# Rows of b2 spread by GpSimd, and a new order of the first twenty microseconds, in a conditional residual kernel

## The chip, the cores and the metric

The kernel runs on one core of a Trainium2 chip. The metric is device time in microseconds of one execution. Three executions of the kernel before took 303.17, 303.27 and 303.47; the median, 303.27, is the time before.

The engines are called as in the profile: PE is TensorE, DVE is VectorE, ACT is ScalarE, POOL is GpSimd, SP is SyncE. A "q" behind a name is that engine's instruction queue (its sequencer), which also issues DMAs.

## The reference

For each of 128 batches there is a tile x[b] of 128 rows and 512 columns, float32, and a language id 0 to 8 that picks one of ten sets of weights.

```python
h = relu(einsum('bsh,bha->bsa', x, W1[lang]) + b1[lang])      # 512 -> 128
adapted = einsum('bsa,bah->bsh', h, W2[lang]) + b2[lang]      # 128 -> 512
y = x + adapted
mean, var = mean(y), var(y)                                   # over the 512 columns
normed = (y - mean) * rsqrt(var + 1e-5)
out = x + normed * gamma[lang] + beta[lang]
```

The ids are data: which row of b2, gamma or beta a batch needs is known on the chip only.

## The kernel before, in words

Each batch is one 128x512 tile, and the main loop goes over batches with its stages shifted against each other. Every instruction is chained behind the one before it on its own engine (`keep`, L46), so the order of the calls in the text is the order on each engine, and a wait holds up all that stands behind it there.

A batch takes these steps:

- `transpose_x` (L264, the matmuls at L271 into pxT): four transposes of x on PE. `copy_xT` (L273) brings them to SBUF by ACT. There is one pxT buffer. The first 17 batches read strided columns.
- `down` (L290, ph at L294): x times W1 on PE, with the batch's W1 in a tile w1s. `relu` (L300) by ACT gives hT.
- `up` (L304, py at L311): h times W2 on PE into one of five y buffers in PSUM (`p_y`, which the rows below use too). For a batch of `b2_by_matmul` one more product (L310) picks its row of b2 out of `parts` and adds it on PE.
- b2 comes in by one of three ways: by that product; by VectorE, which adds the row of the table `b2_b` to y (`vector_b2`, L318, for the batches of `b2_by_vector`); or by GpSimd, which adds it to x beforehand (`add_b2`, L277, tile r). `add_beta` (L283, tile o) adds beta's row to x on GpSimd for every batch.
- `residual` (L323) on VectorE adds x or r to y and sums; `square` on ACT sums squares; `scale` and `finish` (L394, L403) on VectorE apply mean, gamma and the root and write o; `store` sends two batches at a time. A y buffer is free after `finish`, so `up` of batch b + 5 needs `finish` of batch b.

W1 reaches w1s in two ways. For batches 0 to 16 `load_first` (L158) loads the batch's own W1 from DRAM, after reading the id into a register; from batch 17 on, `stage_w1` (L259) copies it on ACT out of `w1`, the whole table, loaded in four parts by `load_w1`. W2 is loaded in two parts (`load_w2`): languages 0 to 2, then 3 to 9; an `up` waits for both. x of batches 0 to 19 comes two batches a load (`load_part`), later four batches a load (`load_x`, in the main loop). DMAs count on eight semaphores in turn, so each issue waits until the eighth load before it has landed.

Before the main loop stands the opening, an order written out by hand (L540 to L581). Beta, gamma and b2, ten rows each, are loaded into `rows`, split into two bf16 parts in `parts`, and spread over all 128 partitions into the tables `beta_b`, `gamma_b`, `b2_b` (10 x 512 columns each) in two ways:

- `spread(r, engine)` (L225): a matmul by a one-hot column writes row r to all partitions of a y buffer, and ACT copies it to the table (L232).
- `four_copies` (L238) makes one tile with the 30 rows in each group of 32 partitions, and `shuffle_rows` (L244) has VectorE spread row r out of it by a shuffle within each group (L247).

Rows 0 to 9 are beta, 10 to 19 gamma, 20 to 29 b2. `spin` runs matmuls on a constant whose result nobody reads. `x_turn` is `transpose_x` and `copy_xT` together. After the loop stands a second order by hand for the last batches.

Of the kernel before, what the change touches and what calls it, by code (L numbers as in the profile page):

```python
# [8 lines left out]
FP = mybir.dt.float32  # L9
# [7 lines left out]
P = 128  # L17
G = 4
# [4 lines left out]
U = 2  # L23
# [3 lines left out]
def cond_resid_kernel(ctx: ExitStack, tc: tile.TileContext, x, itok, W1, b1, W2, b2, gamma, beta, out):  # L27
# [8 lines left out]
    nc = tc.nc  # L36
# [40 lines left out]

    ids = const.tile([1, B], I32, name="ids")
    rows = rp.tile([P, H], FP, tag="r", name="rows")
    b1r = const.tile([L, A], FP, name="b1r")  # L80
    w1 = const.tile([P, L, KC, A], FP, name="w1")
    w2 = const.tile([P, L * H], FP, name="w2")
# [3 lines left out]
    def load_part(lo, hi, engine=nc.sync):  # L86
        dst = xs[lo // G][:, lo % G : lo % G + hi - lo, :]
        keep(engine.dma_start(out=dst, in_=x[lo:hi].rearrange("b s h -> s b h")))
# [2 lines left out]
    keep(nc.vector.memset(warm, 1.0))  # L91

    keep(nc.sync.dma_start(out=ids, in_=itok.rearrange("(o b) -> o b", o=1)))
    keep(nc.scalar.dma_start(out=rows[0:L, :], in_=beta))
    keep(nc.sync.dma_start(out=rows[L : 2 * L, :], in_=gamma))
    keep(nc.scalar.dma_start(out=rows[2 * L : 3 * L, :], in_=b2))
    load_part(0, 2)
    keep(nc.scalar.dma_start(out=b1r, in_=b1))
    keep(nc.scalar.activation(warm, warm, AF.Abs_reciprocal_sqrt))

    def load_w1(k):
        keep(
            nc.sync.dma_start(out=w1[:, :, k, :], in_=W1[:, k * P : (k + 1) * P, :].rearrange("l p a -> p l a"))
        )
# [53 lines left out]
    def load_first(b):  # L158
        w1s[b] = wp.tile([P, KC, A], FP, tag="w1s", name=f"w1s_{b}")
        src = W1[bass.ds(lid(b, ET.SP), 1)].rearrange("o (p k) a -> p (o k a)", k=KC)  # L160
        keep(nc.sync.dma_start(out=w1s[b].rearrange("p k a -> p (k a)"), in_=src))  # L161

    def load_w2(lo, hi):
        dst = w2[:, lo * H : hi * H].rearrange("p (l h) -> p l h", l=hi - lo)
        keep(nc.sync.dma_start(out=dst, in_=W2[lo:hi].rearrange("l a h -> a l h")))
# [1 line left out]
    load_w2(0, 3)  # L167
    load_first(0)
    load_first(1)
    load_part(2, 4)  # L170
    load_first(2)
    load_first(3)
    load_w2(3, L)
    xs[1] = xp.tile([P, G, H], FP, tag="x", name="x_1")
    load_part(4, 6)
# [21 lines left out]
    xs[4] = xp.tile([P, G, H], FP, tag="x", name="x_4")  # L197
    load_part(16, 18)
    load_w1(2)
    load_first(16)  # L200
    load_part(18, 20)
    load_w1(3)

    def upper(lo):

# [14 lines left out]

    beta_b = const.tile([P, L * H], FP, name="beta_b")
    gamma_b = const.tile([P, L * H], FP, name="gamma_b")
    b2_b = const.tile([P, L * H], FP, name="b2_b")

    def spread(r, copier):  # L225
        t = (beta_b, gamma_b, b2_b)[r // L]
        row = p_y.tile([P, H], FP, tag="y", name=f"row_{r}")
        pick_r = pick[:, r : r + 1].to_broadcast([96, P])
        keep(nc.tensor.matmul(row, lhsT=pick_r, rhs=parts[:96, :], start=True, stop=True))  # L229
        dst = t[:, r % L * H : (r % L + 1) * H]  # L230
        if copier is nc.scalar:
            keep(nc.scalar.copy(dst, row))  # L232
        else:
            keep(nc.vector.tensor_copy(dst, row))
# [3 lines left out]
    def four_copies():  # L238
        t = p_y.tile([P, H], FP, tag="y", name="four_p")
        keep(nc.tensor.matmul(t, lhsT=sel, rhs=parts[:96, :], start=True, stop=True))  # L240
        fours[0] = rp.tile([P, H], FP, tag="r", name="four")
        keep(nc.vector.tensor_copy(fours[0], t))

    def shuffle_rows(lo, hi):  # L244
        for r in range(lo, hi):
            t = (beta_b, gamma_b, b2_b)[r // L]
            keep(nc.vector.stream_shuffle(t[:, r % L * H : (r % L + 1) * H], fours[0], [r] * 32))  # L247

    xT, hT, rs, os, ys, ssqs, nmeans, rstds = {}, {}, {}, {}, {}, {}, {}, {}
    phs, pxs, sums = {}, {}, {}  # L250


    def b2_by_matmul(b):
        return b in (0, 1) or b >= B - 2

    def b2_by_vector(b):
        return b in (2, 3, 9, 13, 17, 21) or 24 <= b < B - 8 and (b % 16 in (1, 6, 11) or b % 32 == 30)

    def stage_w1(b):  # L259
        w1s[b] = wp.tile([P, KC, A], FP, tag="w1s", name=f"w1s_{b}")  # L260
# [22 lines left out]
    def add_beta(b):  # L283
        g, j = divmod(b, 2)
        if j == 0:
            os[g] = op.tile([P, 2, H], FP, tag="o", name=f"o_{g}")
        v = lid(b, ET.Pool)
        keep(nc.gpsimd.tensor_tensor(os[g][:, j, :], xb(b), beta_b[:, bass.ds(v * H, H)], ALU.add))  # L288

    def down(b):  # L290
        phs[b] = p_h.tile([P, P], FP, tag="h", name=f"ph_{b}")
        for k in range(KC):
            keep(
                nc.tensor.matmul(  # L294
                    phs[b], lhsT=w1s[b][:, k, :], rhs=xT[b][:, k, :], start=(k == 0), stop=(k == KC - 1)
                )
            )
        del xT[b], w1s[b]
# [110 lines left out]
    def on(b):  # L409
        return 0 <= b < B  # L410
# [125 lines left out]
    def x_turn(b):  # L536
        transpose_x(b)
        copy_xT(b)

    spin(7, H)  # L540
    four_copies()
    spread(10, nc.scalar)
    spin(1, H)
    x_turn(0)
    transpose_b1()
    spread(11, nc.scalar)
    for n in (0, G):
        lid(n, ET.PE)
    shuffle_rows(0, 10)
    x_turn(1)  # L550
    spread(12, nc.scalar)
    spread(13, nc.scalar)
    down(0)
    relu(0)
    spread(14, nc.scalar)
    x_turn(2)
    spread(15, nc.scalar)
    down(1)
    relu(1)
    spread(16, nc.scalar)  # L560
    spread(17, nc.scalar)
    x_turn(3)
    down(2)
    relu(2)
    spread(18, nc.scalar)
    spread(19, nc.scalar)
    add_beta(0)
    add_beta(1)
    spread(20, nc.scalar)
    spread(21, nc.scalar)  # L570
    down(3)
    relu(3)
    spread(22, nc.scalar)
    add_beta(2)
    add_beta(3)
    shuffle_rows(23, 30)
    spin(1, H)
    spin(1, H // 2)
    up(0)
    x_turn(4)  # L580
    up(1)  # L581

    turned = 5
    for i in range(3, B - 6):
        b = i - U - 1
        if b > G and b % G == 2 and b // G + 3 < NG and b // G + 3 >= 5:
            load_x(b // G + 3)
        up_to = i
        if b <= E:
            if turned <= up_to and on(turned):  # L590
                transpose_x(turned)
            add_b2(b + 2)
            if 4 <= b + 2 <= E:
                add_beta(b + 2)
        for n in range(turned, min(B, up_to) + 1):
            if on(n) and (n > turned or b > E):
                transpose_x(n)
            down(n - 1)
            if on(n):
                copy_xT(n)  # L600
            relu(n - 1)
            if on(n + 1) and n + 1 >= FIRST:
                stage_w1(n + 1)
        turned = max(turned, min(B, up_to) + 1)
        if i - U >= 2 and on(i - U):
# [225 lines left out]
```

## Time and profile before

| what | us | where from |
|---|---|---|
| median of three executions | 303.27 | times |
| the profiled execution | 303.5 | times |
| its span | 301.7 | page |
| busy PE, DVE, ACT, POOL | 294.0, 294.1, 278.9, 281.2 | page, part 1 |
| median from issue to landing: x of two batches, w1s, last part of W2 | 7.1, 7.7, 10.1 | page, part 6 |
| longest waits before 25 us: POOL for beta, PE for x, DVE for PE's up | 11.6, 1.0, 1.0 | waits |
| one spread on ACT (L232), one shuffle on DVE (L247) | 0.59, 0.74 | timeline |
| add of 128x512 on POOL, first and last in the loop | 1.27, 1.46 | timeline |

PE's granted clock is 1.0 in the record throughout. Busy time of an instruction includes what overlaps the next one, so a step's cost in a row of equal instructions is the distance between their starts: 0.65 for a shuffle that records 0.74, 1.23 for an add on GpSimd that records 1.27 or more.

### The profile page before, as it was taken

The numbers are of one execution on the slowest core, as the hardware profiler recorded it, in microseconds if no ns is written. First come the engines' busy times: TensorE is split into PE (matmuls) and PEld (weight loads), VectorE is DVE, ScalarE is ACT, GpSimd is POOL, SyncE is SP. The second block draws the span as 40 slices with busy tenths as digits, with TensorE's granted clock in tenths as the row PEclk, the third lists the DMA queues.
The fourth block names the chain that finished last, engine by engine and source line by source line (L and its number), as shares of the span: only waits on it lengthen the run. The fifth ranks groups of instructions, "written<-read, shape, count | busy, mean of one in ns | idle before, by whom it ended". The sixth has DMA issues, their size and how long they took to land.

```text
span 301.7 us, 7025 instructions
## 1 busy us (share of the span) xinstructions
PE 294.0 (97%) x1829; PEld 219.4 (73%) x1829; DVE 294.1 (97%) x785; ACT 278.9 (92%) x770; POOL 281.2 (93%) x236
## 2 busy tenths in 40 slices
PE   7899999999999999999999999999999999999993
PEld 3668777777777777777777777777777777777761
DVE  6979999999999999999999999999999999999996
ACT  5878789999999999999999999999999999999983
POOL 1299998999999999999999999999999999999972
PEclk9999999999999999999999999999999999999999
DMA  6999999986658866766777566778766667872826
GB/s 232 387 387 366 347 339 406 405 298 193 245 223 268 279 225 219 234 234 236 249 276 244 200 231 241 253 237 277 261 191 219 249 228 249 277 258 98 278 93 224
DMA packets 45353, 78.11 MB, mean 259 GB/s; under 512 B 2137, under 2 KB 9316, under 8 KB 45314
## 3 DMA queue, kind: packets, MB, share of 16 engines
q1 hardware_dynamic: 45254, 77.62, 74.4%
q8 instruction: 15, 0.25, 0.4%
q14 instruction: 24, 0.20, 0.2%
q10 hardware_dynamic: 60, 0.05, 0.1%
HBM read 44.11 MB, written 33.55 MB: 257 GB/s over the span
## 4 chain that ended last, share of the span: by engine, by line
PE 89%; DVE 5%; issue 2%; DMA 2%; SPq 0%; POOL 0%; DVEq 0%; POOLq 0%
PE ph L294 36%; PE py L311 35%; PE pxT L271 18%; DMA x<-in_x_dram 2%; DVE py L328 1%; DVE o L488 1%; DVE py L394 1%; PE row L229 1%; DVE n L494 0%; SPq L161 0%; PE py L310 0%; SPq L143 0%; PE idle L529 0%; DVE rstd_of L370 0%; DVEq L826 0%
## 5 line engine op out<-in xcount | busy, mean ns | idle before, releaser
L288 POOL TENSOR_TENSOR o<-x,beta_b 128x512 f32<-128x512 f32 x121 | 163.1, 1380 | 12.6 <-DVE beta_b L247 11.6
L294 PE MATMUL ph<-xT,w1s 128*128 128x128 f32 x1024 | 135.4, 275 | 0.2 <-DMA w1s<-in_L_cond_W_dram 0.2
L311 PE MATMUL py<-w,hT 128*128 x256 | 131.3, 595 | 0.0
L281 POOL TENSOR_TENSOR r<-x,b_b 128x512 f32<-128x512 f32 x92 | 127.1, 1382 | 0.0
L294 PEld LDWEIGHTS ph<-xT,w1s 128*128 128x128 f32 x1024 | 124.9, 192 | 1.9 <-issue 0.9
L271 PEld LDWEIGHTS pxT<-ident,x 128*128 128x128 f32 x512 | 65.9, 149 | 66.6 <-issue 49.9
L394 DVE SCALAR_TENSOR_TENSOR py<-py,nmean,gamma_b 128x512 f32<-128x512 f32 x124 | 93.5, 754 | 0.0
L403 DVE SCALAR_TENSOR_TENSOR o<-py,rstd,o 128x512 f32<-128x512 f32 x116 | 86.8, 748 | 0.0
L351 ACT ACTIVATE sq<-py,sum 128x512 f32<-128x512 f32 x124 | 85.9, 693 | 0.8 <-DVE py L328 0.6
L275 ACT COPY xT<-pxT 128x512 f32<-128x512 f32 x128 | 74.7, 584 | 5.3 <-PE pxT L271 5.1
L271 PE MATMUL pxT<-ident,x 128*128 128x128 f32 x512 | 77.6, 274 | 1.2 <-DMA x<-in_x_dram 1.0
L328 DVE SCALAR_TENSOR_TENSOR py<-py,r 128x512 f32<-128x512 f32 x97 | 67.1, 692 | 0.1
L262 ACT COPY w1s<-w 128x512 f32 x108 | 66.1, 612 | 0.0
L302 ACT ACTIVATE hT<-ph,b1T 128x128 f32<-128x128 f32 x128 | 47.0, 367 | 8.6 <-PE ph L294 4.2
L311 PEld LDWEIGHTS py<-w,hT 128*128 128x128 f32 x256 | 39.1, 192 | 1.5 <-issue 0.7
L351 ACT ACTIVATION_READ_ACCUMULATOR sq<-py,sum 128x1 f32 x124 | 25.1, 202 | 0.0
L328 DVE SCALAR_TENSOR_TENSOR py<-py,x 128x512 f32<-128x512 f32 x31 | 21.7, 699 | 1.8 <-PE py L311 1.0
L321 DVE TENSOR_TENSOR py<-py,b_b 128x512 f32<-128x512 f32 x27 | 18.7, 693 | 0.1
L361 ACT ACTIVATE root<-ssq,eps 128x2 f32<-128x2 f32 x62 | 16.5, 265 | 0.0
L328 DVE DVE_READ_ACCUMULATOR py<-py,r 128x1 f32 x97 | 13.8, 142 | 0.0
L342 ACT ACTIVATE nmean<-sum 128x2 f32<-128x2 f32 x61 | 12.1, 199 | 0.0
L370 DVE SCALAR_TENSOR_TENSOR rstd<-part,root 128x2 f32<-128x2 f32 x62 | 9.4, 152 | 0.0
(73 smaller groups left out, 105.8 us busy)
## 6 DMA issues: line engine op xcount, KB each, us to landing
out_dram<-o SPq DMA_DIRECT2D x62, 512.0 KB, 3.4
x<-in_x_dram SPq DMA_DIRECT2D x27, 1024.0 KB, 6.6
x<-in_x_dram SPq DMA_DIRECT2D x10, 512.0 KB, 7.1
w1s<-in_L_cond_W_dram SPq DMA_DIRECT2D x20, 256.0 KB, 7.7
w<-in_L_cond_W_dram SPq DMA_DIRECT2D x4, 640.0 KB, 8.2
w<-in_L_cond_W_dram SPq DMA_DIRECT2D x1, 1792.0 KB, 10.1
w<-in_L_cond_W_dram SPq DMA_DIRECT2D x1, 768.0 KB, 5.3
out_dram<-o SPq DMA_DIRECT2D x4, 128.0 KB, 1.7
```

The costliest lines, as they stand in the source:

```text
L262: keep(nc.scalar.copy(w1s[b].rearrange("p k a -> p (k a)"), src))
L271: keep(nc.tensor.transpose(pxs[b][:, k, :], cols, ident))
L275: keep(nc.scalar.copy(xT[b], pxs.pop(b)))
L281: keep(nc.gpsimd.tensor_tensor(rs[b], xb(b), b2_b[:, bass.ds(v * H, H)], ALU.add))
L288: keep(nc.gpsimd.tensor_tensor(os[g][:, j, :], xb(b), beta_b[:, bass.ds(v * H, H)], ALU.add))
L294: nc.tensor.matmul(phs[b], lhsT=w1s[b][:, k, :], rhs=xT[b][:, k, :], start=(k == 0), stop=(k == KC - 1))
L302: keep(nc.scalar.activation(hT[b], phs.pop(b), AF.Relu, bias=b1T[:, bass.ds(lid(b, ET.Activation), 1)]))
L311: keep(nc.tensor.matmul(ys[b], lhsT=hT[b], rhs=w2[:, bass.ds(v * H, H)], start=not m, stop=True))
L328: nc.vector.scalar_tensor_tensor(ys[b], ys[b], 1.0, r, ALU.mult, ALU.add, accum_out=col(sums, b))
L351: nc.scalar.activation(sq, ys[b], AF.Square, bias=col(sums, b), scale=-float(H), accum_out=col(ssqs, b))
L394: nc.vector.scalar_tensor_tensor(ys[b], ys[b], col(nmeans, b), gamma_b[:, bass.ds(v * H, H)], ALU.add, ALU.mult)
L403: nc.vector.scalar_tensor_tensor(o, ys[b], rstds[g][:, j : j + 1], o, ALU.mult, ALU.add)
```

## The change

The ten rows of b2 are loaded a second time, as one row of 5120 numbers in partition 0 of `b2_b`, and GpSimd spreads them to all partitions with two `partition_broadcast` instructions of 2560 columns. So `spread` and `shuffle_rows` no longer handle rows 20 to 29. In the built program GpSimd changes its instruction library ahead of the two broadcasts, and changes it back ahead of its first add.

The opening is reordered: x of 0 and 1 is the first load of ACT's queue, and the three loads into `rows` go to SP; x of 2 and 3 is issued behind the w1s of 2 and 3; seven rows go by `spread` (before: thirteen) and thirteen by `shuffle_rows` (before: seventeen); `up` of 0 and 1 both stand ahead of `x_turn(4)`, and `up` of 2 follows it. b2 of batches 0 and 7 is added by VectorE (before: by PE and by GpSimd). In the main loop x of 20 to 23 is issued two batches sooner, ahead of the store of batches 4 and 5. The last part of `w1` is issued ahead of two loads that stood before it. Nothing else of the loop, and nothing of the last order by hand, is touched.

```diff
@@ loads @@
-    keep(nc.scalar.dma_start(out=rows[0:L, :], in_=beta))
+    load_part(0, 2, nc.scalar)
+    keep(nc.sync.dma_start(out=rows[0:L, :], in_=beta))
+    keep(nc.scalar.dma_start(out=b1r, in_=b1))
+    keep(nc.scalar.dma_start(out=b2_b[0:1, :], in_=b2.rearrange("(o l) h -> o (l h)", o=1)))
     keep(nc.sync.dma_start(out=rows[L : 2 * L, :], in_=gamma))
-    keep(nc.scalar.dma_start(out=rows[2 * L : 3 * L, :], in_=b2))
-    load_part(0, 2)
-    keep(nc.scalar.dma_start(out=b1r, in_=b1))
+    keep(nc.sync.dma_start(out=rows[2 * L : 3 * L, :], in_=b2))
...
     load_first(1)
-    load_part(2, 4)
     load_first(2)
     load_first(3)
+    load_part(2, 4)
     load_w2(3, L)
...
     load_w1(2)
+    load_w1(3)
     load_first(16)
     load_part(18, 20)
-    load_w1(3)
@@ b2 @@
+    for half in range(2):
+        cols = slice(half * (L // 2) * H, (half + 1) * (L // 2) * H)
+        keep(nc.gpsimd.partition_broadcast(b2_b[:, cols], b2_b[0:1, cols]))
...
     def b2_by_matmul(b):
-        return b in (0, 1) or b >= B - 2
+        return b in (1,) or b >= B - 2
     def b2_by_vector(b):
-        return b in (2, 3, 9, 13, 17, 21) or 24 <= b < B - 8 and (b % 16 in (1, 6, 11) or b % 32 == 30)
+        return b in (0, 2, 3, 7, 9, 13, 17, 21) or 24 <= b < B - 8 and (b % 16 in (1, 6, 11) or b % 32 == 30)
@@ the opening, as it stands after @@
+    spin(7, H)
+    transpose_b1()
+    for n in (0, G):
+        lid(n, ET.PE)
+    x_turn(0)
+    spin(1, H)
+    spread(2, nc.scalar)
+    four_copies()
+    shuffle_rows(3, 4)
+    spread(0, nc.scalar)
+    shuffle_rows(6, 7)
+    x_turn(1)
+    spread(13, nc.scalar)
+    shuffle_rows(9, 10)
+    shuffle_rows(4, 5)
+    spread(1, nc.scalar)
+    down(0)
+    relu(0)
+    shuffle_rows(17, 18)
+    shuffle_rows(11, 12)
+    shuffle_rows(8, 9)
+    spread(12, nc.scalar)
+    shuffle_rows(7, 8)
+    shuffle_rows(5, 6)
+    add_beta(0)
+    add_beta(1)
+    spin(1, H)
+    x_turn(2)
+    down(1)
+    relu(1)
+    shuffle_rows(18, 19)
+    x_turn(3)
+    shuffle_rows(15, 16)
+    spread(19, nc.scalar)
+    down(2)
+    relu(2)
+    spread(10, nc.scalar)
+    down(3)
+    relu(3)
+    up(0)
+    up(1)
+    x_turn(4)
+    up(2)
+    shuffle_rows(14, 15)
+    add_beta(2)
+    shuffle_rows(16, 17)
@@ the main loop @@
-        if b > G and b % G == 2 and b // G + 3 < NG and b // G + 3 >= 5:
-            load_x(b // G + 3)
+        if b == 8 or b > 12 and b % G == 2 and b // G + 3 < NG:
+            load_x(5 if b == 8 else b // G + 3)
...
-            if 4 <= b + 2 <= E:
+            if 3 <= b + 2 <= E:
                 add_beta(b + 2)
...
-        if i - U >= 2 and on(i - U):
+        if i - U >= 3 and on(i - U):
             up(i - U)
```

More of the change, by code (lines that the diff above doesn't have):

```diff
@@ L79, in cond_resid_kernel @@
     rows = rp.tile([P, H], FP, tag="r", name="rows")
+    b2_b = const.tile([P, L * H], FP, name="b2_b")
     b1r = const.tile([L, A], FP, name="b1r")
@@ L222, in cond_resid_kernel @@
     gamma_b = const.tile([P, L * H], FP, name="gamma_b")
-    b2_b = const.tile([P, L * H], FP, name="b2_b")
     def spread(r, copier):
@@ L540, in cond_resid_kernel @@
     spin(7, H)
[L541 to L544, printed above, removed]
     transpose_b1()
-    spread(11, nc.scalar)
     for n in (0, G):
         lid(n, ET.PE)
-    shuffle_rows(0, 10)
+    x_turn(0)
[5 more added lines that the diff above has]
+    shuffle_rows(6, 7)
     x_turn(1)
-    spread(12, nc.scalar)
     spread(13, nc.scalar)
+    shuffle_rows(9, 10)
+    shuffle_rows(4, 5)
+    spread(1, nc.scalar)
     down(0)
     relu(0)
-    spread(14, nc.scalar)
+    shuffle_rows(17, 18)
[7 more added lines that the diff above has]
+    spin(1, H)
     x_turn(2)
-    spread(15, nc.scalar)
     down(1)
     relu(1)
-    spread(16, nc.scalar)
-    spread(17, nc.scalar)
+    shuffle_rows(18, 19)
     x_turn(3)
+    shuffle_rows(15, 16)
+    spread(19, nc.scalar)
     down(2)
     relu(2)
[L565 to L570, printed above, removed]
+    spread(10, nc.scalar)
     down(3)
     relu(3)
-    spread(22, nc.scalar)
-    add_beta(2)
[L575 to L581, printed above, removed]
+    up(0)
[3 more added lines that the diff above has]
+    shuffle_rows(14, 15)
+    add_beta(2)
+    shuffle_rows(16, 17)
     turned = 5
```

## The prediction

> **What bounds the kernel now.** Times are microseconds from the span's start. I read the busy table first (PE 97%, DVE 97%, ACT 92%, POOL 93%), which names no bound. Then the chain of waits: PE takes 89% of it, and cut to 10 to 24 us it has no gap of another engine:
>
> ```profile
> 4.73 5.58 DMA x<-in_x_dram
> 10.31 0.14 issue
> 10.44 0.72 PE pxT L271 x4
> ...
> 16.58 0.31 PE py L310
> 16.89 0.94 PE py L311 x2
> 17.83 0.71 PE pxT L271 x4
> 18.54 0.22 PE py L310
> 18.76 1.72 PE py L311 x4
> 20.48 0.47 PE pxT L271 x4
> 20.94 0.89 PE ph L294 x8
> ```
>
> Columns: start, length, what. PE waits once for x of batches 2 and 3 (landed at 10.31) and never rests again; from 20.94 on a batch is ph 0.89, py 0.86, pxT 0.47, 2.22 together (2.19 from batch 17 on, where the transposes read whole columns). So the span is the opening up to the ph of batch 4 at 20.94, then 124 steps of a fixed size, then the tail. Only a shift of that 20.94, or a new wait behind it, changes the time.
>
> Next the DMA side, from the table of issues (median to landing) and SyncE's timeline (start, length):
>
> ```profile
> w<-in_L_cond_W_dram SPq DMA_DIRECT2D x1, 1792.0 KB, 10.1
> ```
>
> ```profile
> 1.52 0.41 SPq L88 DMA_DIRECT2D x<-in_x_dram  x1
> 1.97 0.47 SPq L165 DMA_DIRECT2D w<-in_L_cond_W_dram  x1
> 6.24 0.44 SPq L165 DMA_DIRECT2D w<-in_L_cond_W_dram  x1
> 6.72 0.61 SPq L88 DMA_DIRECT2D x<-in_x_dram  x1
> ```
>
> The second part of W2 lands at 6.24 + 10.1 = 16.34, and no up can start before it, whatever PE does. The engines' windows give the DMA 151 GB/s in 0 to 5 us and about 388 from 5 to 25: the queue is full from about 3.3 us on, so a landing moves only with the front of the queue or with its place in it.
>
> Last GpSimd and VectorE, from their timelines:
>
> ```profile
> 13.06 4.98 POOL L288 TENSOR_TENSOR o<-x,beta_b 128x512 f32<-128x512 f32 x4 [11.60 <-DVE beta_b L247]
> ...
> 22.91 1.29 POOL L281 TENSOR_TENSOR r<-x,b_b 128x512 f32<-128x512 f32 x1
> ```
>
> ```profile
> 16.80 0.76 DVE L247 STREAM_SHUFFLE b_b<-four 128x512 f32<-128x512 f32 x1
> ...
> 29.55 0.69 DVE L328 SCALAR_TENSOR_TENSOR py<-py,r 128x512 f32<-128x512 f32 x1
> ```
>
> GpSimd idles until beta is spread (13.06) and then runs without a gap, an add every 1.23 us. It is busy, but ahead: its r of batch 6 ends at 24.20 and VectorE uses it at 29.55, a lead of 5.35. Leads of the same kind are 6.2 at batch 4, 4.8 at batch 8 and 3.8 at batch 90, the least. VectorE is also near full, with five y buffers between it and PE; in the early batches a buffer is free about 0.5 us or more before the up that needs it.
>
> **The change, part by part.**
>
> *The front of the queue.* x of 0 and 1 is issued at about 0.75 (ScalarE's first issue) instead of 1.52: at most 0.77 earlier. Behind it ScalarE issues b1 and the new 20 KB row of b2 (20 KB at 388 GB/s: 0.05). SyncE now issues ids, beta, gamma and b2 ahead of W2's first part: one issue more, so that part starts near 2.2 instead of 1.97. x takes 512 KB / 390 GB/s = 1.3 us to move, which covers the 0.25. The first w1s now waits for x of 0 and 1 to land, because it reuses that load's semaphore (eight go round): about 4.3 instead of 3.77; W2's first 768 KB (2.0 us) cover that, barely. The bounds of the shift are -0.25 (SyncE's later issue sets the front) and 0.77 (all of it); I take 0.65, nearer the upper end since the transfer that opens the queue is the one that moves. W2 then lands at 15.7.
>
> *x of 2 and 3 behind two w1s.* 2 x 256 KB more ahead of it: 1.35 later, less 0.65: 11.0 instead of 10.31. From there PE has pxT 0.47, ph 0.89, pxT 0.47, row 0.22, ph 0.89, row 0.22, ph 0.89 = 4.05, done at 15.05, before W2. So the six spreads taken from PE (13 to 7, 0.22 each), the half spin and the b2 product of batch 0 (0.22) are not counted as such: they let PE be ready, and the landing of W2 takes over as the limit. Without that cover each would be worth its 0.22.
>
> *up of 1 ahead of pxT of 4.* From W2 on: up 0.94, row 0.22, up 0.86, pxT 0.47, up 0.86, pxT 0.47 = 3.82. With 0.05 for the start, ph of batch 4 begins at 15.75 + 3.82 = 19.57 instead of 20.94: **1.37 earlier**. x of 4 and 5, which PE waited for at 17.79 before, lands near 17.1 and is wanted at 17.77. w1s of 4 (landed 18.43 before) is there too.
>
> *VectorE.* parts comes some 0.45 later, since the last of the three row loads is issued at 1.87 on SyncE instead of 1.38; four is copied by 6.7 instead of 5.87. Then 13 shuffles at 0.65 instead of 17, ending at 15.1; the last beta row is the ninth, 12.6. All before the first up ends at 16.7. b2 of batch 0 adds 0.70: 16.7 to 17.4, residuals of 0 and 1 to 19.1, up of 2 ends at 19.1: just covered; uncovered it would cost up to 0.7. b2 of batch 7 is 0.70 more where VectorE runs 0.11 behind PE; batch 9 makes the same step today (0.77 behind) and PE does not wait; the 0.5 of free buffers hides it, 0.2 per batch is caught up.
>
> *The broadcasts.* No row shows one. The b2 row, behind x on ScalarE's queue, lands near 4.6. Each broadcast writes 2560 elements per partition. From rows: memset of 128x128 against 128x1 (0.20, 0.10) is 0.8 ns an element, 4.2 us for both; the two-input add (1.27 for 512) is 2.5 ns, 12.7 us for both. The select of ident, one input, is 1.5 ns; between it and the memset I take 6 us. They end at 10.6, and 17.3 at worst. The instruction needs another GpSimd library, changed ahead of the broadcasts and back ahead of the first add. The row on such a change:
>
> ```profile
> masks.py:199 POOLq MODIFY_POOL_CONFIG  x2: 11/11/11, 1.1 to 1.1; - x2
> ```
>
> 11 ns, and the select begins 0.06 after it. It may ask for a library that is already there, so it bounds the change from below only; from above the nearest row is ScalarE's table load, 1.28. I take a few tenths. GpSimd then starts adding when beta is there, at 12.7 as before, with one add less (batch 7). When would it hurt? The lead of 5.35 less the 1.4 that PE gains: free until 13.06 + 5.35 - 1.4 = 17.0, 0.5 more for the y buffers, then one for one; at 18.9 the whole gain is gone. Later batches allow more (batch 90: 3.8, plus 1.23 for batch 7, plus a wait of 1.0 for a store at 46 us that a late GpSimd absorbs).
>
> Here the Trainium skill speaks against the change: its page "GPSIMD Engine Reference", section 2.1, says the first call to a freshly loaded kernel also pays a load of about 6 us (5.95 measured) that the profile shows as no instruction. The trace neither confirms nor excludes it, since it holds no change to a library that was not there. An estimate by that page: 1.5 + 5.95, 6 for the broadcasts, 5.95 back, adds from 19.4, and the time 303.8.
>
> *x of 20 and w1.* x of 20 to 23 was issued at 43.09 and landed near 53.2, with the transposes of 20 at 53.53: 0.3 to spare. Moved ahead of one 512 KB store it lands 1.3 + 0.65 earlier, PE wants it 1.37 earlier: 0.9 to spare. The store it passes (landed near 50) frees an output buffer that GpSimd next writes at 56. w1's last part passes w1s of 16 and x of 18, which come 640 KB, 1.6 us, later and had over 5 to spare. Nothing.
>
> **Sum.** 301.7 - 1.4 = 300.3. The profiled execution took 303.5, 1.8 beside its span, and lies 0.23 above the median of 303.27; on the median the forecast is **301.9**.
>
> **Rivals.**
> *The front does not move* (SyncE's issue order holds it): W2 lands at 16.34, gain 0.7, 302.6. For it: the w1s that waits; against: 1.3 us of x as cover. 0.08.
> *x of 20 does not come sooner*, so PE waits at 53 us and keeps 0.3 of the gain: 303.0. For it: the queue is full to 60 us; against: its place in the queue. 0.07.
> *GpSimd starts late*: place, the first add of beta after the broadcasts; it decides from 18.9 on. Two-input speed for the broadcasts and a table load's 1.28 at each library change: 4.6 + 12.7 + 2.6 = 19.9; VectorE waits at the r of batch 6, 19.9 - 17.5 = 2.4 less 1.4: 1.0 slower, 304.3. For it: no row shows the operation, both library changes are new, the DMA is full while code would load; against: the configuration row and the one-input rates. 0.33, of which 0.05 lands within 0.6 us of before.
>
> **How the numbers follow.** The forecast has 0.52. Within 0.2% (0.6 us) is what the measurement cannot tell from no change. Faster: 0.52 + 0.08 = 0.60; same: 0.07 + 0.05 = 0.12; slower: 0.28. The forecast's own range, with the shift from -0.25 to 0.77 and 0.3 for the covers, is 301.4 to 302.8; stretched over the late GpSimd it is 301.4 to 304.4, leaving out a still later GpSimd and little else.
>
> **What would show it.** Right: first up near 15.7, ph of batch 4 near 19.6, steps of 2.22 and 2.19 after it without a PE gap, GpSimd's first beta add near 12.7. Wrong: an empty stretch on GpSimd around the broadcasts, beta adds from 17 on, VectorE waiting for r at batches 4 to 8; or W2 landing at 16.3; or PE waiting for x at batch 20.

## The result, and the profile after

The changed kernel takes 313.14 us, the median of five executions (312.73 to 313.92), beside 303.47 for the kernel before on the same chip: 9.7 us more (9.9 between the two profiled spans, 311.6 and 301.7), a ratio of 1.0324 with a 95% interval of 1.0313 to 1.0335. The forecast of 301.9 was wrong, and its range of 301.4 to 304.4 too.

In the chain of work that ended last PE had 89%. It now has 58%, and VectorE, GpSimd and time without a visible cause ("issue") stand in the rest:

```profile
PE 58%; DVE 13%; POOL 13%; issue 10%; DMA 1%; POOLq 1%; ACT 1%; DVEq 0%; SPq 0%; ACTq 0%
```

Where the 9.7 us lie is seen on GpSimd first. Its timeline in the changed kernel (start, length, what; in brackets the idle time before it and the event that ended nearest to its end):

```profile
1.41 0.29 POOL masks.py:199 TENSOR_SCALAR_AFFINE_SELECT ident<-ident 128x128 f32<-128x128 f32 x1 [0.29 <-POOL eps L113]
9.72 5.48 POOL L252 PARTITION_BROADCAST b_b<-b_b  x2 [8.02 <-DVE four L243]
25.93 4.94 POOL L293 TENSOR_TENSOR o<-x,beta_b 128x512 f32<-128x512 f32 x4 [10.73 <-ACT sq L356]
30.83 1.25 POOL L286 TENSOR_TENSOR r<-x,b_b 128x512 f32<-128x512 f32 x1
```

The two broadcasts take 5.48, near the 6 of the forecast. But GpSimd stands empty for 8.02 ahead of them and for 10.73 behind them, and its first add of beta begins at 25.93, where it began at 13.06 before. The names in the brackets mislead: `four` and `sq` have nothing to do with GpSimd. The row of the instruction that changes the library says nothing either, since it is as short as it was before:

```profile
L252 POOLq MODIFY_POOL_CONFIG  x2: 11/11/11, 1.7 to 1.7; - x2
```

The waits of 14 to 45 us (engine and line, whom it waited for: total, times, longest) tell who pays:

```profile
POOL o L293 <- ACT sq L356: 10.7, 1, 10.7
ACT sq L356 <- DVE py L333: 5.5, 1, 5.5
DVE py L333 <- POOL r L286: 4.8, 3, 4.1
...
PE py L316 <- DVE part L372: 3.7, 1, 3.7
```

VectorE's residual of batch 4 needs `r` from GpSimd. It is ready at 32.08 and used at 32.12, a lead of 0.03 where the kernel before had 6.2. ACT's square stands behind VectorE, no y buffer comes free, and PE waits. PE's timeline and the windows (start:end, then for PE, PEld, DVE, ACT and POOL the busy time and instructions, PE's granted clock, DMA share, GB/s) show a second thing:

```profile
29.45 1.06 PE L299 MATMUL ph<-xT,w1s 128*128 128x128 f32 x8
34.26 2.07 PE L316 MATMUL py<-w,hT 128*128 x2 [3.75 <-DVE part L372]
36.12 1.06 PE L276 MATMUL pxT<-ident,x 128*128 128x128 f32 x4
36.98 1.91 PE L299 MATMUL ph<-xT,w1s 128*128 128x128 f32 x8
38.68 1.61 PE L316 MATMUL py<-w,hT 128*128 x2
40.13 0.63 PE L276 MATMUL pxT<-ident,x 128*128 128x128 f32 x4
```

```profile
32.00:34.00 2.00, 0.00 (x0) 0.00 (x0) 1.88 (x5) 1.09 (x3) 2.00 (x3) 0.76 1.05 379
34.00:36.00 2.00, 1.74 (x2) 0.73 (x3) 1.70 (x7) 1.07 (x4) 2.00 (x3) 0.50 1.13 302
36.00:38.00 2.00, 2.00 (x10) 1.88 (x9) 1.65 (x5) 1.02 (x5) 2.00 (x2) 0.50 0.22 56
38.00:40.00 2.00, 2.00 (x7) 1.25 (x6) 1.10 (x3) 1.04 (x3) 2.00 (x3) 0.54 0.03 9
40.00:42.00 2.00, 2.00 (x15) 1.63 (x14) 1.67 (x6) 0.90 (x3) 2.00 (x3) 1.00 0.93 312
```

PE is empty for 3.75, and from 33 to just before 40 us its granted clock is 0.50, so that an up takes 2.07 instead of 1.02. (The Trainium skill, "TensorE: Matmul & The Clock Gate", part 1, gives half the clock behind an idle window of about 3.4 us. This trace agrees so far that the clock falls within a wait of 3.75. But it fell as well behind waits of 1.90 in e7_library_alone and 1.79 in e12_back_in_ten, and not behind one of 2.65 in e5_loads_back; no run here shows a limit of 3.4.) By the transposes of batch 10, at 40.13 instead of 31.42, the main loop is 8.71 late, and it stays so to the end (8.68 at batch 127). The last 1.2 us come in the tail. There GpSimd is the one that is late. Before, and after, each time GpSimd's r of batch 123, VectorE's residual of that batch, which reads it, and GpSimd's two products of gamma:

```profile
283.93 1.50 POOL L427 TENSOR_TENSOR r<-x,b_b 128x512 f32<-128x512 f32 x1
...
286.65 0.69 DVE L328 SCALAR_TENSOR_TENSOR py<-py,r 128x512 f32<-128x512 f32 x1
...
289.57 1.27 POOL L454 TENSOR_TENSOR n<-n,gamma_b 128x512 f32<-128x512 f32 x1 [0.45 <-ACT n L439]
...
293.61 1.27 POOL L454 TENSOR_TENSOR n<-n,gamma_b 128x512 f32<-128x512 f32 x1 [1.42 <-ACT n L439]
```

```profile
294.77 1.26 POOL L432 TENSOR_TENSOR r<-x,b_b 128x512 f32<-128x512 f32 x1
...
296.06 0.70 DVE L333 SCALAR_TENSOR_TENSOR py<-py,r 128x512 f32<-128x512 f32 x1 [0.64 <-POOL r L432]
...
299.69 1.26 POOL L459 TENSOR_TENSOR n<-n,gamma_b 128x512 f32<-128x512 f32 x1
...
303.02 1.27 POOL L459 TENSOR_TENSOR n<-n,gamma_b 128x512 f32<-128x512 f32 x1 [0.73 <-ACT n L444]
```

In the kernel before, r of batch 123 was ready 1.22 ahead of its use (285.43 and 286.65). That is the shortest lead in the whole kernel; it lies in the order by hand behind the loop. GpSimd is 12.87 late at its first add. The add that it no longer makes for batch 7 gives back 1.2, and a wait for a store at 46 us that the kernel before has gives 1.07; 10.6 are left at r of batch 123. Less the lead of 1.22 this is 9.4, and VectorE's residual is 9.41 late, its last instruction 9.40 (307.56 instead of 298.16). The other 0.5 of the 9.9 lie behind that instruction, as in e1_memset below; no run explains them.

The front of the DMA queue is the other surprise. The DMA's GB/s over 0 to 8 us in 40 slices of 0.2, and what was moved in all, before and after:

```profile
GB/s 0 0 0 0 0 0 0 0 95 10 102 92 10 82 0 20 358 430 361 466 358 445 351 348 246 338 389 430 358 369 338 440 369 440 369 451 369 430 389 410
DMA packets 1049, 1.93 MB, mean 242 GB/s; under 512 B 97, under 2 KB 108, under 8 KB 1049
```

```profile
GB/s 0 0 0 0 0 0 0 0 3 102 256 184 276 410 399 420 399 359 231 41 41 72 31 72 205 246 358 379 420 399 420 399 420 287 318 297 420 369 410 369
DMA packets 969, 1.80 MB, mean 225 GB/s; under 512 B 90, under 2 KB 101, under 8 KB 968
```

The queue is full 0.6 us sooner (400 GB/s from 2.6 instead of 358 from 3.2), as forecast, but from 3.8 to 4.8 it falls to 31 to 72 GB/s, and by 8 us less has been moved than before, 1.80 MB instead of 1.93. The row loads now come behind x, and VectorE waits 3.15 for the last of them:

```profile
6.41 0.68 DVE L210 TENSOR_TENSOR rows<-rows 30x512 f32<-30x512 f32 x1 [3.15 <-DMA rows<-in_L_cond_b_dram]
```

`parts` is ready at 7.81 instead of 4.50, and PE reaches the transposes of batch 2 at 12.98 instead of 10.44 and the ph of batch 4 at 21.55 instead of 20.78. PE was not only later there, but slower too. The ph of batch 0, before and after:

```profile
8.09 1.13 PE L294 MATMUL ph<-xT,w1s 128*128 128x128 f32 x8 [0.18 <-DMA w1s<-in_L_cond_W_dram]
```

```profile
10.83 1.88 PE L299 MATMUL ph<-xT,w1s 128*128 128x128 f32 x8
```

From 6.6 to 12.5 a matmul of 512 columns takes 0.61 to 0.63 in the changed kernel, and 0.38 before. In e1_memset it takes 0.63 as well where the granted clock reads 0.50 (7.1 to 10.4); the changed kernel's own record of the clock begins only at 12.5. What keeps the clock low there is not shown. x of 2 and 3 had landed at 12.41, so PE came 0.6 behind it, and its first up at 17.66 stands 0.5 behind the landing of W2 (17.14).

### The profile page after: what moved, and what is told of

It reads as the page before. It is cut to its first block, busy times and chain, and to the rows that moved or that the text cites. A ratio compares the mean times of both kernels' runs of the same rounds, so it can differ in the third digit from the quotient of the medians.

```text
span 311.6 us, 7005 instructions
## 1 busy us (share of the span) xinstructions
PE 298.1 (96%) x1821; PEld 221.9 (71%) x1821; DVE 292.6 (94%) x779; ACT 276.1 (89%) x764; POOL 285.3 (92%) x237
## 4 chain that ended last, share of the span: by engine, by line
PE 58%; DVE 13%; POOL 13%; issue 10%; DMA 1%; POOLq 1%; ACT 1%; DVEq 0%; SPq 0%; ACTq 0%
PE ph L299 23%; PE py L316 22%; PE pxT L276 12%; POOL o L293 6%; POOL r L286 5%; DVE py L399 4%; DVE py L333 3%; DVE o L408 2%; DMA rows<-in_L_cond_b_dram 1%; POOL o L428 1%; DVE py L326 1%; POOL r L432 1%; POOLq L145 1%; DVE o L493 1%; PE row L230 1%
## 5 line engine op out<-in xcount | busy, mean ns | idle before, releaser
L293 POOL TENSOR_TENSOR o<-x,beta_b 128x512 f32<-128x512 f32 x121 | 152.5, 1269 | 10.7 <-ACT sq L356 10.7
L299 PE MATMUL ph<-xT,w1s 128*128 128x128 f32 x1024 | 137.2, 278 | 0.7 <-ACT hT L307 0.7
L316 PE MATMUL py<-w,hT 128*128 x256 | 133.2, 602 | 4.7 <-DVE part L372 3.7
L299 PEld LDWEIGHTS ph<-xT,w1s 128*128 128x128 f32 x1024 | 126.6, 194 | 2.8 <-ACT hT L307 2.0
L286 POOL TENSOR_TENSOR r<-x,b_b 128x512 f32<-128x512 f32 x91 | 115.6, 1270 | 0.0
L276 PEld LDWEIGHTS pxT<-ident,x 128*128 128x128 f32 x512 | 66.6, 150 | 67.0 <-issue 51.0
L276 PE MATMUL pxT<-ident,x 128*128 128x128 f32 x512 | 78.9, 277 | 0.8 <-issue 0.8
L333 DVE SCALAR_TENSOR_TENSOR py<-py,r 128x512 f32<-128x512 f32 x96 | 66.1, 688 | 5.4 <-POOL r L286 4.8
L326 DVE TENSOR_TENSOR py<-py,b_b 128x512 f32<-128x512 f32 x29 | 20.0, 688 | 2.2 <-PE py L316 2.1
L252 POOL PARTITION_BROADCAST b_b<-b_b x2 | 5.5, 2800 | 8.0 <-DVE four L243 8.0
```

What stands on the lines that cost most here:

```text
L276: keep(nc.tensor.transpose(pxs[b][:, k, :], cols, ident))
L286: keep(nc.gpsimd.tensor_tensor(rs[b], xb(b), b2_b[:, bass.ds(v * H, H)], ALU.add))
L299: nc.tensor.matmul(phs[b], lhsT=w1s[b][:, k, :], rhs=xT[b][:, k, :], start=(k == 0), stop=(k == KC - 1))
L316: keep(nc.tensor.matmul(ys[b], lhsT=hT[b], rhs=w2[:, bass.ds(v * H, H)], start=not m, stop=True))
L333: nc.vector.scalar_tensor_tensor(ys[b], ys[b], 1.0, r, ALU.mult, ALU.add, accum_out=col(sums, b))
```

## The experiments

### Which part of GpSimd's lateness: the changes of the library, or the broadcasts

**e1_memset.** The changed kernel with two memsets of the same size in the place of the broadcasts, so that no library is changed; b2 is left out wherever VectorE or GpSimd adds it.

```diff
-        keep(nc.gpsimd.partition_broadcast(b2_b[:, cols], b2_b[0:1, cols]))
+        keep(nc.gpsimd.memset(b2_b[:, cols], 0.0))
```

> The changed kernel with its two broadcasts replaced by two GpSimd memsets of the same 128x2560, so GpSimd changes no library; the load of the b2 row stays. Left out: b2 in every batch where VectorE or GpSimd adds it (the table holds zeros). Theory A (the two library changes hold GpSimd, 8.0 us ahead of the broadcasts and 10.7 behind them, and that costs most of the 9.7): the first add of beta starts when beta is spread, near 15.6 instead of 25.9; no wait for r; what stays is the later ph of batch 4 (21.7 against 20.9), so 304.0 to 304.5. Theory B (the reordered opening itself costs it): above 308.

Measured: 304.50 (304.03 to 305.12), a ratio of 1.0042, interval 1.0026 to 1.0059. GpSimd's timeline:

```profile
5.28 4.40 POOL L252 MEMSET b_b<- 128x2560 f32 x2 [3.82 <-DMA b_b<-in_L_cond_b_dram]
14.84 4.96 POOL L293 TENSOR_TENSOR o<-x,beta_b 128x512 f32<-128x512 f32 x4 [5.16 <-ACT hT L307]
```

GpSimd is idle only for its data. The first add is at 14.84, `r` of batches 4 to 6 is 3.5 to 4.4 ahead, and 8.6 of the 9.7 us are gone. What is left, 1.1, shows that the rest of the change gains nothing: the ph of batch 4 begins at 20.75 against 20.78 before. In the profiled execution, the fastest (304.03), the loop is 0.1 late at its end and the span 0.6 longer, the rest of it behind the last instruction.

**e7_library_alone.** The other way round: the kernel before with nothing but two changes of the library.

```diff
+    small = const.tile([P, 16], FP, name="small")
+    keep(nc.gpsimd.memset(small, 0.0))
+    keep(nc.gpsimd.partition_broadcast(small[:, 8:16], small[0:1, 0:8]))
```

> The kernel before with a memset of 16 columns and one partition_broadcast of 8 columns added on GpSimd in the opening, whose result nothing reads. Nothing else is changed. Theory (the two changes of GpSimd's library cost the time, not the length of the broadcasts and not the new order): GpSimd's first add of beta begins at 19 to 21.5 instead of 13.06, behind two empty stretches of 8 to 10; VectorE waits for r at batches 4 to 8, and the time is 304.3 to 306.5, more if the granted clock of PE drops in that wait. Rival (the broadcasts' 5.5 and the reordered opening cost it, the changes alone end before beta is there): first add before 17, time within 0.6 of before.

Measured: 309.72 (308.94 to 310.77), a ratio of 1.0202, interval 1.0180 to 1.0224. On GpSimd:

```profile
10.40 0.28 POOL L251 PARTITION_BROADCAST small<-small  x1 [8.66 <-issue]
20.91 4.96 POOL L292 TENSOR_TENSOR o<-x,beta_b 128x512 f32<-128x512 f32 x4 [10.23 <-DVE py L332]
```

The empty stretches are there with a broadcast of 0.28: 8.66 and 10.23, 18.9 together. Up to 12.96 GpSimd would have waited for beta anyway; its first add is 7.85 late. So it is the changes and not the length of the broadcasts. The cost, 6.3, is above what was expected when only the wait for `r` was reckoned with. The trace shows why: the loop is 2.5 late by batch 14 and 3.0 at the end, the other 3.7 come in the tail. VectorE's residual of batch 123 waits for r and is 5.2 late; PE stands 1.90 behind that, and its granted clock, 1.00 from 24 to 294 us, falls to 0.60 from 294 to 296 and 0.55 from 296 to 298:

```profile
294.07 1.82 PE L298 MATMUL ph<-xT,w1s 128*128 128x128 f32 x8 [1.90 <-ACT hT L306]
295.68 1.92 PE L315 MATMUL py<-w,hT 128*128 x2
```

VectorE's last instruction is 6.7 late, so about 1.5 of the cost arise where the clock is low.

**e4_quiet.** The price of a change where nothing else runs: three pairs of a small broadcast and a small add behind GpSimd's last instruction of the kernel before.

```diff
+    q = const.tile([P, 32], FP, name="q")
+    keep(nc.gpsimd.memset(q, 1.0))
+    for j in range(3):
+        keep(nc.gpsimd.partition_broadcast(q[:, 8:16], q[0:1, 0:8]))
+        keep(nc.gpsimd.tensor_tensor(q[:, 16:24], q[:, 8:16], q[:, 0:8], ALU.add))
```

> The kernel before, with three pairs of a broadcast of 8 columns and an add of 8 columns put behind GpSimd's last instruction: six library changes, the later ones with no load or store in flight. If a library change is a load of fixed length, each pair shows two gaps like the 8.0 and 10.7 of the opening. If the full DMA queues of the opening stretched it, the later gaps are shorter, about 6 or less. If the change is free where it was not the cause, gaps under 0.5.

Measured, one execution: 339.99. On GpSimd:

```profile
302.62 0.28 POOL L798 PARTITION_BROADCAST q<-q  x1 [6.44 <-issue]
309.81 0.20 POOL L799 TENSOR_TENSOR q<-q 128x8 f32<-128x8 f32 x1 [6.91 <-issue]
315.96 0.28 POOL L798 PARTITION_BROADCAST q<-q  x1 [5.96 <-issue]
323.21 0.19 POOL L799 TENSOR_TENSOR q<-q 128x8 f32<-128x8 f32 x1 [6.97 <-issue]
```

A change costs about 6 in and 7 back, the second time as the first (the third pair: 5.96 and 7.55). In the opening, under a full DMA queue, the same changes took 8.0 to 8.9 and 9.3 to 10.7. That the full queue stretches them is the likely reading; no run took the load off the queue in the opening.

**e3_row_in_ten.** Whether the broadcasts only wait for their row: the long row of b2, written in the kernel as ten pieces of 2 KB.

```diff
-    keep(nc.scalar.dma_start(out=b2_b[0:1, :], in_=b2.rearrange("(o l) h -> o (l h)", o=1)))
+    keep(nc.scalar.dma_start(out=b2_b[0:1, :].rearrange("o (l h) -> o l h", l=L), in_=b2.rearrange("(o l) h -> o l h", o=1)))
```

> The changed kernel with the b2 row loaded as ten pieces of 2 KB, so on ten DMA engines; broadcasts and library changes stay, the output is whole. If the library changes set the time, the opening on PE moves by up to 0.8 but GpSimd's first add stays near 25.9 and the time within 0.6 of 313.1. If the broadcast's start at 9.7 was the row's late landing and not the library, it starts 3 or more us sooner and the time falls by 3 or more.

Measured: 313.78 (313.21 to 314.12). The broadcasts begin at 10.04 and the first add at 25.71, as before the edit. But the edit did not cut the load: the trace still has one packet of 20480 bytes for it (0.81 us long, at 3.78). This run is the changed kernel once more and settles nothing. That the row is not what the broadcasts wait for is seen elsewhere: in the changed kernel its packet lies at 3.75 and takes 1.84, so it is done 4.1 before the first broadcast begins, and e7_library_alone loads no such row.

### Why a late GpSimd costs so much

My forecast let a late GpSimd be free as long as the lead of `r` over its use was not used up. The tails above say where it is used up: GpSimd's stream of adds runs almost without a gap into the last batches, and with the lead of 1.22 at batch 123 it is a second bound of the whole kernel.

**e13_two_adds.** Two more adds on GpSimd in the middle of the kernel before, far from the opening.

```diff
+    unread = const.tile([P, H], FP, name="unread")
...
+            if b == 60:
+                for _ in range(2):
+                    keep(nc.gpsimd.tensor_tensor(unread, beta_b[:, :H], gamma_b[:, :H], ALU.add))
             add_b2(b + 2)
```

> The kernel before with two more adds of 128x512 on GpSimd ahead of its adds of batch 62, into a tile that nothing reads; nothing else is changed. Theory (GpSimd's stream of adds is a second bound of the whole kernel: it runs gap-free into the tail, where before shows one spare wait of 0.45 and one of 1.4 behind it): its adds from there on and the first gamma product of the tail come 2.46 - 0.45 = 2.0 later, and the time is 304.7 to 305.6. Rival (the rule of my forecast: a late GpSimd is free while the lead of its r, 3.8 at batch 90, is not used up): leads of 1.3 at batch 90, no wait for r, time within 0.6 of before.

Measured: 304.90 (304.64 to 305.08), a ratio of 1.0048, interval 1.0035 to 1.0062, so 1.5 more. The loop on PE is where it was (0.2 earlier at batch 127), and VectorE waits only in the tail. GpSimd's r of batches 123 and 124, VectorE's residual of 123, and VectorE's waits for r from 262 us on:

```profile
286.81 2.62 POOL L429 TENSOR_TENSOR r<-x,b_b 128x512 f32<-128x512 f32 x2
...
288.24 0.70 DVE L330 SCALAR_TENSOR_TENSOR py<-py,r 128x512 f32<-128x512 f32 x1 [0.69 <-POOL r L429]
```

```profile
DVE py L330 <- POOL r L429: 1.7, 2, 1.0
```

r of batch 123 is 2.8 late (288.20 instead of 285.43). The lead of 1.22 takes its part, and the residual is 1.59 late (288.24 instead of 286.65), as is VectorE's last instruction. A late GpSimd is free only up to the shortest lead that follows, and that is this one, not the 3.8 of batch 90.

**e10_library_three.** Less for GpSimd to do where it is late: e7_library_alone with three batches of b2 handed to PE.

```diff
     def b2_by_matmul(b):
-        return b in (0, 1) or b >= B - 2
+        return b in (0, 1, 56, 68, 84) or b >= B - 2
```

> The kernel of e7_library_alone with b2 of batches 56, 68 and 84 added by PE instead of GpSimd: three adds of 1.23 less on GpSimd, three products of 0.22 more on PE. Theory (in e7_library_alone the main loop is 3.0 later and GpSimd 6.45 later, and GpSimd's 3.5 beyond the loop are paid in the tail): GpSimd is 2.8 late at the end, less than the loop's 3.0 + 0.66, and the time falls from 309.7 to 306.8 to 307.8. Rival (the tail is late for another reason than GpSimd): PE's 0.66 come on top, 310.2 to 310.6.

Measured: 306.83 (305.44 to 308.50), 2.9 less than e7_library_alone. GpSimd is 2.3 late at batch 115 and the loop 2.9; VectorE no longer waits for r in the tail, PE's clock stays at 1.00 there, and GpSimd's waits ahead of its products of gamma are back at 1.17 and 1.42. So the 3.7 us in e7_library_alone's tail came from GpSimd being late, the fall of the clock with them.

### PE's clock: two misses

The clock of 0.50 stretches the changed kernel's batches 6 to 8 by some 2.9 (in the chain of work py, pxT, ph, py take 2.06, 0.85, 1.71, 1.40 instead of 0.86, 0.47, 0.89, 0.86). Whether the whole kernel pays for it I tried with matmuls that nothing reads, ahead of the up of batch 6.

```diff
+        if i - U == 6:
+            warm_px = p_x.tile([P, KC, P], FP, tag="xT", name="warm_px").rearrange("p k a -> p (k a)")
+            for _ in range(16):
+                keep(
+                    nc.tensor.matmul(
+                        warm_px, lhsT=ones, rhs=ones[:, 0:1].to_broadcast([P, H]), start=True, stop=True
+                    )
+                )
```

**e8_kept_warm.** 

> The changed kernel with 16 more matmuls on a constant, whose result nothing reads, on PE ahead of up of batch 6, where PE waits for GpSimd's late r. Theory (of the 9.7, some 2 to 2.9 come from the granted clock of PE, which falls to 0.5 from 33 to 40 us after PE stood idle): the clock stays near 1.0 from 33 to 40 us, the steps of batches 7 to 9 fall to 2.2 as GpSimd allows, and the time is 310.8 to 311.6. Rival (GpSimd alone sets the batches behind the wait, whatever PE's clock): the clock stays up and the time stays within 0.5 of 313.1.

**e9_warm** has 64 matmuls of 128 columns into unused columns of the ph tile of batch 7 in their place. 

> The changed kernel with 64 matmuls of 128 columns on a constant ahead of up of batch 6, into unused columns of the ph tile of batch 7, so that they run in PE's wait and not behind it (as those of e8_kept_warm did). Theory (GpSimd's stream sets the end, the fall of PE's clock only the middle): the clock stays near 1.0 from 32 to 40 us and the transposes of batch 10 begin 1.8 to 2.5 earlier, at 37.6 to 38.3, but the time stays within 0.7 of 313.1, the tail paying what the loop gained. Rival (the clock costs its 2.9 of the whole): 310.6 to 311.4.

**e11_warm_three** is e9_warm with b2 of batches 56, 68 and 84 by PE. 

> The kernel of e9_warm with b2 of batches 56, 68 and 84 added by PE instead of GpSimd. Theory (GpSimd's stream sets the end): GpSimd 10.8 - 3.7 = 7.1 late at batch 115, the loop 8.7 - 2.3 + 0.66 = 7.1 late, time 310.4 to 311.4, and the clock now counts. Rival (the tail is not set by GpSimd): no less than e9_warm, whatever that is, and 0.66 more.

Measured: 314.41 (313.94 to 314.80), 314.80 (314.32 to 316.48) and 315.22 (314.87 to 316.25). In e8_kept_warm and e9_warm the added matmuls waited themselves, for ACT's copy and for its relu, both of which stand behind the late square:

```profile
33.93 5.31 PE L618 MATMUL warm_px<-ones 128*128 128x512 bf16 x16 [2.85 <-ACT xT L280]
```

```profile
34.15 5.01 PE L621 MATMUL ph_wide<-ones 128*128 128x128 bf16 x64 [3.97 <-ACT hT L312]
```

So they ran behind the wait, at the low clock (0.50 from 34 to 36 in e9_warm), and made the loop 10.8 and 10.7 late. Nothing follows for the clock's own price. One thing follows from e11_warm_three: with three adds less on GpSimd the loop is still 10.9 late and the time does not fall, while GpSimd's waits in the tail are back (1.97 and 1.42). There the loop sets the end. Two chains stand side by side, and the later one is the time: the loop, and GpSimd's lateness at batch 123 less the lead of 1.22. Reckoned so, VectorE's last instruction comes out to 0.1 in the changed kernel (9.4 by GpSimd, 8.7 by the loop), e10_library_three (the loop's 2.9), e13_two_adds (1.6 by GpSimd) and the three runs here (the loop); in e7_library_alone the clock adds its 1.5 to GpSimd's 5.2. In the changed kernel GpSimd runs without a gap from 25.93 to that r, so the low clock from 33 to 40 us does not move it and would be covered. That is argued; the clock's price by itself was not measured.

### The front of the DMA queue: misses that show how fragile it is

**e5_loads_back.** e1_memset with the first loads ordered as before and the long row last on ScalarE's queue.

```diff
-    load_part(0, 2, nc.scalar)
-    keep(nc.sync.dma_start(out=rows[0:L, :], in_=beta))
+    keep(nc.scalar.dma_start(out=rows[0:L, :], in_=beta))
+    keep(nc.sync.dma_start(out=rows[L : 2 * L, :], in_=gamma))
+    keep(nc.scalar.dma_start(out=rows[2 * L : 3 * L, :], in_=b2))
+    load_part(0, 2)
...
-    keep(nc.sync.dma_start(out=rows[L : 2 * L, :], in_=gamma))
-    keep(nc.sync.dma_start(out=rows[2 * L : 3 * L, :], in_=b2))
```

> The kernel of e1_memset (changed kernel with two memsets of 128x2560 in the place of the two broadcasts, so b2 is left out wherever VectorE or GpSimd adds it), with the first loads as they were before: beta, b2 and b1 on ScalarE's queue, ids, gamma and x of 0 and 1 on SyncE's, and the long row of b2 last on ScalarE's. Theory (the front of the DMA queue was made later by x of 0 and 1 going first on ScalarE's queue, since the row loads then wait behind it): the wait of VectorE for rows falls from 2.5 to below 1, W2's second part lands near 16.4, ph of batch 4 begins at 20.2 to 20.3 instead of 20.75, and the time is 0.3 to 0.7 below e1_memset: 303.8 to 304.2. Rival (the order of the first loads sets nothing, since W2's place in the full queue sets its landing): ph of batch 4 stays within 0.15 of 20.75 and the time within 0.2 of e1_memset.

Measured: 306.62 (304.75 to 307.60). The rows came early, as expected: VectorE takes them at 3.10, with no wait. The loop is 2.5 late all the same, because PE stood 2.65 for x of 2 and 3 in the profiled execution:

```profile
14.14 0.72 PE L276 MATMUL pxT<-ident,x 128*128 128x128 f32 x4 [2.65 <-DMA x<-in_x_dram]
```

Fifteen of the sixteen parts of that load had landed by 12.10, the last at 14.01.

**e12_back_in_ten.** e5_loads_back with the edit of e3_row_in_ten. 

> The kernel of e5_loads_back (memsets in the place of the broadcasts, so b2 is left out wherever VectorE or GpSimd adds it; first loads as before) with the long row of b2 loaded in ten pieces of 2 KB instead of one of 20 KB. In e5_loads_back the rows came early as expected (no wait of VectorE for them), but one of the sixteen parts of x of 2 and 3 landed at 14.01, the others by 12.10. Theory (the one packet of 20 KB holds up the one DMA engine that carries it): all parts land by 12.2, the transposes of batch 2 begin at 11.5 to 12.3 instead of 14.14, ph of batch 4 ends at 21.6 to 22.0 and the time is 303.0 to 304.2. Rival (the late part has another cause, such as small loads of ScalarE's queue behind x): the last part stays at 13.5 or later and the time within 0.5 of 306.6.

Measured: 304.99 (304.00 to 306.88). The row is one packet of 20480 bytes here too (1.59 us long, at 4.42), so this is e5_loads_back once more, and the two together show how far such a front scatters: 304.0 to 307.6. The profiled execution, one of the slowest at 306.64, has a late last part as well (13.14, the others by 12.31), and behind PE's wait of 1.79 a clock of 0.50 from 14 to 17.3. Whether the 20 KB packet delays that sixteenth was not tested by either run and stays open.

**e6_x_first.** The front alone in the kernel before: x of 0 and 1 first, on SyncE.

```diff
+    load_part(0, 2)
     keep(nc.sync.dma_start(out=ids, in_=itok.rearrange("(o b) -> o b", o=1)))
     keep(nc.scalar.dma_start(out=rows[0:L, :], in_=beta))
-    keep(nc.sync.dma_start(out=rows[L : 2 * L, :], in_=gamma))
+    keep(nc.scalar.dma_start(out=rows[L : 2 * L, :], in_=gamma))
     keep(nc.scalar.dma_start(out=rows[2 * L : 3 * L, :], in_=b2))
-    load_part(0, 2)
```

> The kernel before with one thing moved: x of 0 and 1 is the first load of SyncE's queue, ahead of ids, and gamma goes to ScalarE's queue behind beta. Theory (x of 0 and 1 at 0.7 instead of 1.5 starts the full queue earlier and moves W2, as my forecast had it): W2's second part lands 0.5 to 0.8 earlier, ph of batch 4 begins at 20.0 to 20.3, time 302.6 to 302.9. Rival (what the changed kernel showed: the small row loads wait behind x, parts and with them the gamma and b2 rows come later, and W2 lands no sooner): parts 1 to 3 later, ph of batch 4 at 20.8 or later, time 303.3 to 305.

Measured: 306.58 (304.98 to 307.47), a ratio of 1.0102, interval 1.0077 to 1.0126. The ids stand behind x, and all the addresses behind the ids:

```profile
4.40 0.21 DVE L135 TENSOR_SCALAR wrap<-ids 1x128 int32<-1x128 int32 x1 [2.06 <-DMA ids<-in_itok_B_dram]
```

The first w1s is issued at 5.92 instead of 3.77, W2's second part lands at 17.89 instead of 16.38, and the loop is 2.1 late. The rival had the cause right, though the time is above its 305: moving 512 KB ahead of a few small loads costs more than it gains, since the small loads are what the next big ones wait for. About 0.6 of the 2.1 are not W2's. PE's matmuls of 512 columns take 0.61 to 0.63 until 12 us here as well, and PE reaches the transposes of batch 2 at 12.90, 1.2 behind the landing of their x (11.69).

**e2_memset_norow.** e1_memset without the long row's load, so b2 is left out there as well.

```diff
-    keep(nc.scalar.dma_start(out=b2_b[0:1, :], in_=b2.rearrange("(o l) h -> o (l h)", o=1)))
```

> As the kernel with memsets, and the load of the b2 row is taken away too. Left out: the same b2. Theory A1 (the row is one packet of 20 KB, 1.84 us on one DMA engine, and the last load into rows waits behind it): that load lands near 4.7 instead of 6.3, the second part of W2 near 16.3 instead of 17.0, ph of batch 4 starts 0.5 to 0.8 sooner, time 303.2 to 303.8. Rival (it is the three row loads on SyncE that wait behind the x on ScalarE's queue): landing and time as in the kernel with memsets, within 0.2.

Measured: 306.97 (306.55 to 307.73). It settles nothing: with no row to wait for, the memset of 2.23 ran ahead of GpSimd's select of ident (at 3.33 instead of 1.17), the ids were prepared later, and the first w1s was issued at 7.46 instead of 4.39.

## Why the prediction was wrong, step by step

**The step that failed: the library changes.** The forecast took "a few tenths" each, bounded above by ScalarE's table load of 1.28. They cost 8.0 and 10.7, and e7_library_alone shows 8.7 and 10.2 without any of the rest. The last row of beta, forecast for 12.6, was spread at 15.64, 2.7 later than before; the first add came 10.3 behind that. The row that I bounded from below with (11 ns) is the issue of the change; its execution is no instruction in the trace and appears as idle time. The rival *GpSimd starts late* had the place right (the first add behind the broadcasts) and mis-sized this term: 2 x 1.28 against 18.7. The Trainium skill, "GPSIMD Engine Reference", section 2.1, whose 5.95 I set aside, was the nearer price: e4_quiet measures 5.96 with the rest of the chip at rest. The estimate from it, adds from 19.4, was still 6.5 short, since both changes took longer in the opening.

**The second step that failed: what a late GpSimd costs.** "Free until 17.0", then 0.5 of buffers, then one for one, was read from the leads of `r`, with 3.8 at batch 90 as "the least". With the first add at 25.93 that gives 25.93 - 17.5 - 1.4 = 7.0 over the time before; it was 9.7. The rule was sound and the reading was not: the least lead of the kernel before is 1.22, at batch 123, in the order by hand. From it, 12.87 less 1.2 (batch 7), 1.07 (the wait at 46 us) and 1.22 is 9.4, which is what VectorE's last instruction shows. e13_two_adds, with 3.8 to spare at batch 90, cost 1.5. I should have followed the leads to the last batch.

**The front of the queue** failed as well. It was to come 0.65 earlier, but W2's second part landed at 17.14, 0.76 later than the 16.38 of the kernel before. x of 0 and 1 did land 0.8 earlier (4.21 instead of 5.05), but I took it that 1.3 us of x cover the small loads behind it, and 1 us of an almost empty queue followed. `parts` was to be 0.45 later and was 3.3 later. x of 2 and 3, forecast for 11.0, landed at 12.41 and was transposed at 12.98, since PE was slow until 12.5, a term that the forecast does not have; PE then took 4.7 instead of 4.05 to the first up, at 17.66 instead of 15.7. So W2 no longer covered the opening's own work. In e1_memset this costs nothing against before (20.75 against 20.78) and takes away the gain of 1.37; in the changed kernel ph of batch 4 is 0.77 late.

**Right** were the up of 0 and 1 ahead of the transposes of 4 (first up to ph of batch 4 3.89, forecast 3.82), the broadcasts (5.48, forecast 6) and, in e1_memset, b2 of 0 and 7 by VectorE: PE's steps behind batch 4 are 2.22 as before. Whether x of 20 comes in time for an earlier loop could not be seen, since the loop was never earlier.

## What to carry to other kernels

Before giving GpSimd an operation of another kind, look for a change of its library: it costs some 6 to 11 us each way, the trace shows it as idle time under a foreign name, and one lone call in a kernel pays it twice. The slack of an engine that runs gap-free is the gaps that it has left and the shortest lead of all that follows, the last batches included, not the lead at the point where it is late. A large load moved to the front moves past every small one that the next loads wait for. And whether an edit of a load changed the transfer is seen in its packets: the ten pieces went as one.

No version that was run beats the kernel before.

## What was not expected of the hardware

- A change of GpSimd's library costs the way back as well, and more: 5.96 in, 6.91 to 7.55 back with the DMA at rest; 8.0 to 8.9 and 9.3 to 10.7 in the opening.
- `partition_broadcast` of 2560 columns takes 2.80, 1.1 ns a column; of 8 columns 0.28. A memset of the same size takes 2.23.
- A wait of PE of 3.75 brought nearly 7 us at half the clock, from 33 to 40 us; waits of 1.79 (e12_back_in_ten) and 1.90 (e7_library_alone) brought over 3 us of it, and one of 2.65 (e5_loads_back) none.
- In the changed kernel's opening PE's matmuls took about 1.7 times as long as before (0.63 against 0.38) until 12.5 us.
- A hole of 1 us at 31 to 72 GB/s opened in a queue that had been full at 400. e2_memset_norow, without the long row, still falls to 51 GB/s; the cause was not tested.
